# Layer 2's self attention in skewed steps with the norm by tile, and new arrangements of the mixtures' heads and of layer 1's weight rounding

## The chip, the cores and the metric

One core of a Trainium2 chip runs the whole program: four layers, each of a cross attention, a self attention and a feed-forward part, twelve stages in all. The metric is the device time of one execution in microseconds (us), lower is better; a time of the kernel is the median of several executions. The engines of the core run side by side and wait for each other by semaphores: PE (TensorE, matrix products and transposes; PEld is its weight load), DVE (VectorE), ACT (ScalarE), POOL (GpSimd) and SP (SyncE, which here only issues transfers). Each engine takes its instructions in order.

## What is computed

`x` has 16 x 64 tokens of 256 features, that is 1024 rows, and there is a context of 16 x 1601 rows. Every stage is `x = x + stage(layernorm(x), ...)`. The stages that the change touches are these:

```python
# layer 2, self attention (64 tokens of a batch see each other, causally)
q, k, v = x @ Wq, x @ Wk, x @ Wv
att = softmax(where(causal, q @ k.T / sqrt(256), -inf))
out = layer_norm(att @ v + v, gamma, beta)
return out @ Wfc + bfc
# layers 0 and 3: two of eight experts for each token; layer 2: one of eight
logits = x @ Wg.T            # layer 2: (x @ wg_red.T) @ unit(wg).T
gates, experts = top_k(softmax(logits))
out[token] += gate * expert(x[token])
# layer 1, feed-forward: weights and activations rounded
w1q, w2q = round(w1 / mean|w1|), round(w2 / mean|w2|)   # clipped to -1, 0, 1
y = bit_linear(silu(conv(bit_linear(x, w1q))), w2q)
```

## The kernel before

The 1024 rows lie as eight tiles of 128 rows (`NT = 8`), `self.x` and its normed copy `self.xn`. `run` (L2348) goes through the twelve stages; ahead of each it asks for the weights of this stage and of the next, afterwards it calls `normalise()`. The writer gives the instructions in program order, and a scheduler at build time sets the order on each engine. An instruction that goes through `pinned` (L193) while `self.fixed` is set stays behind everything written before it on its engine; others may move ahead. All PE work passes through `mm` (matrix product, L199) or `tr` (transpose, L203), so PE's rows carry one of these two lines.

**The norm.** When a stage has finished tile `t` of `x`, `ready(t)` (L299) takes mean and variance on DVE (`bn_stats`, `bn_aggr`), three small operations on POOL make the scale and the shift (L309 to L311, one of them a power), and `normalise` writes `xn` on ACT (L317), one tile later than it was measured. After the experts of a mixture all eight tiles come back from memory at once and `ready` runs for each in turn (L1591).

**Layer 2's self attention** (L1344) is written tile by tile without pins. All queries and keys are projected first; then for each tile: values, scores, maximum, exponential, transpose of the probabilities, product with the values. Then all eight outputs are normed (`layernorm`, L279), turned (`to_T`) and multiplied with `Wfc`.

**The head of a mixture.** `expert_rows` (L1593) stores `xn` in memory with one transfer and turns all of it; `gate_logits` (L1436) multiplies each tile with the gates; `top2`, `two_choices`, `places` and `slots` work out on DVE in which expert tile and row each token goes. `places` counts with a running sum of 16 additions (L1454), `slots` compares with a list of 128 row numbers 16 times (`R`, L1518) for 16 products on PE. `experts` (L1531) then has for each of 23 (layer 2: 15) expert tiles the weights `W` (three buffers, loaded by SP at an address read from `rows`), the tokens `xs` gathered by POOL from memory, two products, and a scattered addition to memory by POOL (L1578), one after the other. In this kernel the first three `W` are asked for as soon as `rows` is known.

**Layer 1's rounding.** `quant_weight` (L1766) rounds a weight matrix of 128 x 2048 numbers: a sum of absolute values on DVE (L1772), one small product, and three passes on ACT and DVE. For `w1` it is written as a whole at step 165 of layer 1's cross attention, which runs 227 steps of one key tile each; for `w2` in layer 1's self attention (L1336), into whose weight buffer `w2` is loaded at its start. The context tiles `ctxT` of the cross attentions go through two buffers of the pool `stream`.

## Time and profile before

| what | value |
|---|---|
| median of 3 runs | 3267.34 us (3263.81 to 3276.09) |
| the profiled execution | 3270.24 us, its span 3268.5 us |
| busy PE / ACT / DVE / POOL | 93% / 42% / 39% / 11% |
| granted PE clock, mean over the span | 0.952 |
| layer 1's cross attention, with its projections | 844 to 1699 us |
| layer 1's self attention, feed-forward | 1699 to 1773, 1773 to 1864 us |
| layer 2's cross attention, self attention | 1864 to 2366, 2366 to 2433.5 us |
| the head of layer 0's / 2's / 3's mixture | 602 to 652 / 2433.5 to 2469 / 3043.5 to 3082.3 us |
| the experts of layer 0 / 2 / 3 | 652 to 844 / 2469 to 2581 / 3082.3 to 3253 us |

The times of the stages are counted from the span's start, by where PE passes from one to the next. "Granted clock" is the share of its full rate at which PE was let run. In the profile's rows a name is `out<-in`, a row of the timeline is start, length, engine, line and operation, and the bracket at its end is the idle time of the engine before it and what ended it. A row of the stage table has the length, then for each engine its busy time and number of instructions, then the granted clock, the share of the DMA engines in use and GB/s. DMA is a transfer between memory and the chip.

### The profile page before, as it was taken

Reading aid. Unit: us, or ns where it says so; the run is one execution under the profiler, and the core shown is the slowest. Engines: PE = TensorE matmul, PEld = TensorE weight load, DVE = VectorE, ACT = ScalarE, POOL = GpSimd, SP = SyncE. Lnnn points to the kernel's source line nnn. Section 1 sums busy time; section 2 is a strip of 40 time slices with the busy share of each in tenths; the row PEclk is TensorE's granted clock in tenths of the full one; section 3 lists DMA queues with packets and bytes.
Section 4 is the critical chain, followed back from the end, with each engine's and each line's share of the span. In section 5 each row is a group of like instructions: output and inputs, shape, how many; then the busy total and the mean of one; then the engine's idle time right before and its main releaser. Section 6 shows DMA issues by size and latency. Waiting matters only on the chain. (4 is left out here: it accounts for less than half of the span.)

```text
span 3268.5 us, 67442 instructions
## 1 busy us (share of the span) xinstructions
PE 3028.5 (93%) x28567; PEld 2267.5 (69%) x28567; DVE 1261.3 (39%) x3415; ACT 1361.5 (42%) x2699; POOL 370.9 (11%) x538
## 2 busy tenths in 40 slices
PE   7999997699799999999998999999979798889798
PEld 5666664599566666666676777777748676778697
DVE  6888874422244444444446421121242100045200
ACT  5888884211233333333334522222222387753111
POOL 0000002223200000000010000000012311111132
PEclk9999998699899999999998999999988899999799
DMA  6334431389211121211257111111208555510497
GB/s 217 107 128 135 134 108 42 147 282 322 59 61 61 61 81 43 79 61 61 81 172 224 28 61 41 61 50 52 77 17 302 159 184 183 184 48 1 156 324 241
DMA packets 178362, 395.09 MB, mean 121 GB/s; under 512 B 11446, under 2 KB 142270, under 8 KB 165214
## 3 DMA queue, kind: packets, MB, share of 16 engines
q1 hardware_dynamic: 165070, 372.91, 33.1%
q0 software_dynamic: 11712, 16.00, 2.5%
q8 instruction: 225, 3.69, 0.5%
q10 hardware_dynamic: 1280, 1.88, 0.2%
q14 instruction: 75, 0.61, 0.1%
HBM read 375.02 MB, written 16.12 MB: 120 GB/s over the span
## 5 line engine op out<-in xcount | busy, mean ns | idle before, releaser
L199 PE MATMUL acc<-ctx,st 128*128 128x257 f32 (+1 forms) x1664 | 397.2, 383 | 0.0
L199 PE MATMUL pss<-qk,ctxT 128*128 128x512 f32 (+1 forms) x832 | 388.8, 592 | 0.6 <-DVE qk L634 0.6
L199 PEld LDWEIGHTS acc<-ctx,st 128*128 128x128 f32 (+1 forms) x1664 | 310.1, 190 | 94.6 <-issue 35.7
L459 DVE CUSTOM_DVE_ANT_0 Sx<-s,mneg 128x384 f32<-128x384 f32 (+1 forms) x512 | 264.2, 570 | 88.7 <-PE s L199 88.7
L650 DVE TENSOR_TENSOR top<-pss,top 128x512 f32<-128x512 f32 x192 | 132.7, 691 | 402.4 <-ACT st L645 402.3
L203 PE MATMUL pst<-cst,Sx 128*128 128x128 f32 (+1 forms) x1736 | 254.8, 286 | 26.1 <-ACT Sx L1381 10.2
L674 ACT ACTIVATE st<-st 128x512 f32<-128x512 f32 (+1 forms) x208 | 130.6, 629 | 292.4 <-DVE st L673 292.4
L935 ACT ACTIVATE Pr<-pss 128x512 f32<-128x512 f32 (+1 forms) x512 | 220.1, 523 | 60.2 <-PE pss L199 58.7
L503 ACT ACTIVATE PT<-pst 128x384 f32<-128x384 f32 x512 | 215.1, 489 | 63.6 <-PE pst L203 62.5
L203 PEld LDWEIGHTS pst<-cst,Sx 128*128 128x128 f32 (+1 forms) x1736 | 187.9, 142 | 73.6 <-ACT PT L503 27.8
L199 PEld LDWEIGHTS pss<-qk,ctxT 128*128 128x128 f32 (+1 forms) x832 | 154.1, 186 | 120.7 <-issue 102.7
L645 ACT COPY st<-pss 128x512 f32<-128x512 f32 (+1 forms) x208 | 121.6, 585 | 201.6 <-PE pss L199 201.6
L199 PE MATMUL pso<-W,hT 128*128 128x256 f32 x884 | 200.9, 379 | 0.0
L199 PE MATMUL pst<-wst,ctxT 128*128 128x256 f32 (+1 forms) x832 | 183.4, 380 | 0.0
L199 PE MATMUL psk<-ctxT,wst 128*128 128x512 f32 (+1 forms) x512 | 181.8, 513 | 0.8 <-ACT qT L797 0.8
L199 PEld LDWEIGHTS pso<-W,hT 128*128 128x128 f32 x884 | 163.2, 190 | 19.7
L199 PEld LDWEIGHTS pst<-wst,ctxT 128*128 128x128 f32 (+1 forms) x832 | 153.5, 186 | 25.9 <-issue 2.7
L199 PE MATMUL pss<-q,ctxT 32*128 32x128 f32 (+1 forms) x3328 | 152.2, 299 | 15.9 <-issue 13.1
L199 PEld LDWEIGHTS psk<-ctxT,wst 128*128 128x128 f32 x512 | 88.3, 190 | 93.7 <-issue 92.1
L199 PEld LDWEIGHTS pss<-q,ctxT 32*128 32x128 f32 (+1 forms) x3328 | 120.0, 193 | 47.8 <-issue 36.9
L356 POOL TENSOR_TENSOR x<-x,bvec 128x256 f32<-128x256 f32 x40 | 29.7, 744 | 1079.7 <-ACT xn L317 1079.7
L837 DVE TENSOR_TENSOR v<-pst,bvec 128x512 f32<-128x512 f32 (+1 forms) x112 | 73.1, 653 | 204.4 <-PE pst L199 204.4
(394 smaller groups left out, 4515.9 us busy)
## 6 DMA issues: line engine op xcount, KB each, us to landing
ctxT<-in_ctxT_dram SPq DMA_DIRECT2D x64, 1601.0 KB
W<-in_L_experts_dram SPq DMA_DIRECT2D x61, 1024.0 KB
ctx<-in_ctx_dram SPq DMA_DIRECT2D x32, 1536.0 KB
W<-in_L_experts_dram SPq DMA_DIRECT2D x23, 1536.0 KB
ctx<-in_ctx_ones_dram SPq DMA_DIRECT2D x16, 1632.0 KB
ctx<-in_ctx_one_dram SPq DMA_DIRECT2D x16, 1542.0 KB
W<-in_L_experts_dram SPq DMA_DIRECT2D x23, 768.0 KB
W<-in_L_experts_dram SPq DMA_DIRECT2D x15, 1028.0 KB
```

The source lines that it names most:

```text
L199: self.pinned(self.nc.tensor.matmul(out, lhsT, rhs, start=start, stop=stop))
L203: self.pinned(self.nc.tensor.transpose(out, in_, self.ident[:n, :n]))
L356: self.nc.gpsimd.tensor_tensor(self.x[:, t, :], self.x[:, t, :], self.bv(i), ALU.add)
L459: self.pinned(nc.vector.tensor_tensor_reduce(out=Sx[:, j, :n], in0=ps[j][:, :n], in1=st["mneg"][:, o : o + n], op0=ALU.add, op1=ALU.max, s ...
L503: self.pinned(nc.scalar.activation(PT, ps, AF.Exp))
L645: pin(nc.scalar.copy(st[:kn], ps[:kn]))
L650: pin(nc.vector.tensor_tensor(top[b][:kn], ps[:kn], top[b][:kn], ALU.max))
L674: pin(nc.scalar.activation(st, st, AF.Exp, scale=HD**-0.5))
L837: nc.vector.tensor_tensor(o, ps[:kn, :n, :], bv[:kn].to_broadcast([kn, n, D]), ALU.add)
L935: nc.scalar.activation(st["Pr"][:kn, g : g + n, j, :], ps[j][:kn, :n, :], AF.Silu)
```

## The change

1. `L2_attn` is written in 13 steps with lags and with its instructions pinned: in step `n` the scores of tile `n`, the last product of tile `n-5`, turning of `n-4`, norm of `n-3`, attention of `n-2`, transposing of `n-1`, values of tile `n`. The norm is by tile (POOL has three small operations for each). Transposes, projections and `add_bias` are pinned too.
2. `ready_all` norms the eight tiles after the experts of layers 0 and 2: two powers of four columns on POOL, and the writing of `xn` shared by ACT and DVE.
3. `gate_logits` goes tile by tile: store of the tile (eight transfers), turning, logits a step later. The last tile's `normalise` moves into it, at its fourth step; in front of layer 1's feed-forward it moves behind the first turning.
4. `top2` and `places` write in place (no copies), the running sum takes four doubling steps (three in layer 2), and `slots` makes `R` four at a time.
5. In `experts` only the first `W` is asked for at once; the row numbers of the others are read from `rest`, a copy made by POOL behind the first two gathers.
6. `quant_parts` spreads the five parts of a rounding over steps of layer 1's cross attention: `w1` from step 145, `w2` from step 203. `w2` is loaded there at step 196, into a `ctxT` buffer, which it keeps until layer 1's feed-forward is over. `add_bias(2)` moves to step 3.

```diff
+    def ready_all(self):
+        for h in range(2):
...
+            for i in range(4):
+                pin(nc.vector.bn_stats(st, self.x[:, 4 * h + i, :]))
+                pin(nc.vector.bn_aggr(mv[:, i, :], st))
+            pin(nc.vector.tensor_scalar(rs[:, 0], mv[:, :, 1], 1e-5, None, ALU.add))
+            nc.gpsimd.tensor_tensor(
+                rs[:, 0], rs[:, 0], self.c("pow")[:, 0:1].to_broadcast([P, 4]), ALU.pow)
+        for h, (mv, rs) in enumerate(parts):
+            pin(nc.vector.scalar_tensor_tensor(
+                rs[:, 1], mv[:, :, 0], -1.0, rs[:, 0], ALU.mult, ALU.mult))
+            for i in range(4):
+                if i % 2:
+                    pin(nc.vector.tensor_scalar(o, x, ...))
+                else:
+                    pin(nc.scalar.activation(o, x, AF.Identity, ...))
...
@@ L1_xattn
-                self.add_bias(2)
+                at(3, self.add_bias, 2)
-                    at(NKT * 12 + 9, self.quant_weight, pst, self.w1, "pst")
+                    for i, part in enumerate(self.quant_parts(pst, self.w1, "pst")):
+                        at(NKT * 11 + 2 + 2 * i, part)
+                    at(NKT * 15 + 1, self.load_w2)
+                    def ready_w2():
+                        for i, part in enumerate(self.quant_parts(pst, self.w2, "pst")):
+                            at(NKT * 15 + 8 + 2 * i, part)
+                    at(NKT * 15 + 7, ready_w2)
@@ L1_attn
-                        if n == 3:
-                            self.quant_weight(psa, self.held["L1_ffn"][1], "py")
@@ L2_attn
+            tc.tile_pool(name="l2a_t", bufs=4, space=PSUM) as pst,
+            tc.tile_pool(name="l2a_v", bufs=2, space=PSUM) as psv,
+            tc.tile_pool(name="l2a_o", bufs=1, space=PSUM) as pso,
+            self.fixed = True
...
+            for n in range(NT + 5):
+                for lag, fn in (
+                    (0, scores), (5, last), (4, back), (3, normal), (2, attend), (1, turn),
+                    (0, values),
+                ):
+                    if 0 <= n - lag < NT:
+                        fn(n - lag)
@@ places
-        for g in range(G):
-            nc.vector.tensor_tensor(cum[:, g + 1, :], cum[:, g, :], ps[:, g, :], ALU.add)
+        nc.vector.tensor_copy(cum[0][:, pad:, :], ps)
+        while step < G:
+            nc.vector.tensor_tensor(
+                cum[1][:, pad:, :], cum[0][:, pad:, :], cum[0][:, pad - step : pad - step + G, :],
+                ALU.add)
+            cum.reverse()
+            step *= 2
@@ slots
-        for g in range(G):
-            nc.vector.tensor_scalar(R, self.c("iota128"), lo[:, g : g + 1], None, ALU.is_equal)
-            self.mm(ps, R, V[:, :, g, :], g == 0, g == G - 1)
+        for g in range(0, G, 4):
+            nc.vector.tensor_tensor(R, ..., ALU.is_equal)      # 128 x 4 x 128
+            for i in range(4):
+                self.mm(ps, R[:, i, :], V[:, :, g + i, :], g + i == 0, g + i == G - 1)
@@ experts
-        got = [fetch(0), fetch(1)]
+        W, xs = {0: fetch(0, rows)}, [gather(0), gather(1)]
+        self.pinned(nc.gpsimd.tensor_copy(rest, rows))
+        W[1] = fetch(1, rest)
...
-            for t in range(NT):
-                self.ready(t)
+            self.ready_all()
@@ gate_logits
+        def turn(t):
+            nc.sync.dma_start(xin[t * P : (t + 1) * P, :], self.xn[:, t, :])
+            for kc in range(2):
+                self.tr(ps[:, kc, :], self.xn[:, t, kc * P : (kc + 1) * P])
+            pin(nc.scalar.copy(turned[t], ps))
...
+        for t in range(NT + 2):
+            if t < NT:
+                turn(t)
+            if 0 <= t - 1 < NT:
+                logits(t - 1)
+            if 0 <= t - 2 < NT:
+                reduced(t - 2)          # layer 2 alone: the second, small product
+            if t == 3:
+                self.normalise()
@@ L1_ffn
             turn_x(0)
+            self.normalise()
@@ run
-                self.normalise()
+                if after not in ("L0_ffn", "L1_ffn", "L2_ffn", "L3_ffn"):
+                    self.normalise()
```

## The prediction

> **What bounds the kernel now.** First the page: PE is busy for nearly all of the span, and the slices show where it isn't.
>
> ```profile
> PE 3028.5 (93%) x28567; PEld 2267.5 (69%) x28567; DVE 1261.3 (39%) x3415; ACT 1361.5 (42%) x2699; POOL 370.9 (11%) x538
> PE   7999997699799999999998999999979798889798
> PEclk9999998699899999999998999999988899999799
> ```
>
> 240 us of the span are without PE work, and the dips of both rows (slices of 82 us) lie at the mixtures' heads and in layer 2's self attention. So a saving counts where PE waits, and a change in layer 1's cross attention must only not disturb. Next, the stage table: length, then busy time of PE, weight load, DVE, ACT, POOL, then clock, DMA share, GB/s.
>
> ```profile
> 602.00:652.00 50.00, 25.75 (x179) 22.81 (x178) 24.52 (x95) 7.11 (x15) 8.81 (x18) 0.62 0.61 228
> 881.00:1699.00 818.00, 814.72 (x3554) 537.62 (x3552) 347.11 (x636) 299.90 (x522) 14.56 (x28) 1.00 0.21 69
> 2384.50:2433.50 49.00, 32.79 (x129) 25.57 (x128) 27.54 (x90) 8.44 (x28) 5.47 (x13) 0.79 0.00 0
> 2439.50:2444.00 4.50, 4.16 (x10) 1.36 (x11) 0.84 (x2) 0.94 (x2) 0.00 (x0) 0.50 0.80 262
> 2890.00:3043.50 153.50, 142.16 (x826) 121.09 (x817) 77.30 (x212) 59.89 (x127) 22.47 (x47) 0.97 0.00 1
> 3043.50:3082.30 38.80, 17.27 (x85) 16.04 (x85) 18.28 (x86) 3.26 (x5) 5.54 (x8) 0.56 0.60 226
> 3075.00:3082.00 7.00, 0.00 (x0) 0.00 (x0) 0.00 (x0) 0.00 (x0) 3.24 (x3) 0.50 1.01 416
> ```
>
> The heads of layers 0 and 3 keep PE half idle at a clock near 0.6; layer 2's tile loop waits for a third of 49 us at 0.79. Who it waits for, by the tile `Sx`:
>
> ```profile
>   DVE nm L1379: 24.0, 7
>   ACT Sx L1381: 22.1, 16
> ```
>
> Within a tile everything is a chain: scores, maximum, exponential, transpose, product. The period is 3.92 us, of which PE works 1.9.
>
> **Layer 2's self attention.** At full clock the trace has for a tile: values 0.87, scores 0.43, transpose 0.18, attention 0.43, two transposes 0.36, last product 0.87, in all 3.14 us (25.1 for eight tiles). ACT has 3.1 a step (exponential 0.58, norm 0.52, two turned copies 0.66, probabilities 0.27, values 0.37, waits between), DVE 2.85. Every product reads what an earlier step made, so a full step costs the larger plus little, 3.3. There are 13 steps: five of filling, whose chain scores, maximum, exponential takes 2.1 each (10.6), three full (9.9), five of emptying, in which the last tile goes through attention, statistics, POOL's 1.0, norm, turning and product (10): 30.5 us. I add 1.3 for a clock of 0.95 and 1.8 for 13 hand-overs of 0.14 (0.06 to 0.3 in the trace). Projections now end at 2383.04; pinned behind all transposes, whose last tile comes at 2369.8, they lose 1.0: 2384.05. PE so ends at 2417.6 instead of 2433.35: **15.7 us**. Of the new waits, `normal` on ACT waits for POOL, and behind it stand PT and the values' copy; POOL's three operations (1.01) follow a step earlier, with 1 us to spare. `add_bias` (8 x 0.72 on POOL) is done before step 5 needs `x`.
>
> A rule speaks against it. The row: the clock is 0.79 in the chained loop, 0.97 in layer 3's self attention, where PE is busy 142 of 153 us in skewed steps. The Trainium skill (TensorE: Matmul & The Clock Gate, "A second HAM failure mode: psum-queue depth-cycling") says that micro-idling between groups of products, with accumulators cycled in every iteration, is enough to make the clock oscillate. By the row the products cost 25.1 / 0.95 = 26.4 us, by the rule at 0.79 31.8, so 5.4 less gain: 10.3. At half clock throughout (50 us of products and 5 of waits) nothing is gained, the lower end; the upper, at full clock without hand-overs, is 18.8. I take the row: the new loop is of that form.
>
> **The heads of the mixtures.** Layer 3's, from the timeline (start, length), and its running sum:
>
> ```profile
> 3065.28 4.75 SPq L1545 DMA_DIRECT2D W<-in_L_experts_dram  x6
> 3067.05 7.09 PE L199 MATMUL pst<-V,R 128*128 128x69 f32 x32 [8.21 <-POOL V L1508]
> 3075.14 1.20 POOL L1547 DMA_INDIRECT xs<-l3i,token  x1 [8.15 <-DVE share L1528]
> 3082.28 0.66 PE L203 MATMUL pst<-cst,xs 128*128 128x128 f32 x2 [8.14 <-DMA xs<-l3i,token]
> ```
> ```profile
> L1454 DVE TENSOR_TENSOR cum<-cum,pst x16: 154/161/164, 3058.5 to 3061.5; 128x8 f32<-128x8 f32 x16
> ```
>
> The gather takes 7.1 us because three `W` of 2.1 MB fill the DMA engines (share 1.01 above). With one `W`, 5 us from about 3067, they are free when it starts; the next gather, at 3083.79, landed in 2.75, layer 2's third in 3.01. I take 3.4: **3.7**. Bounds: 0 if something else fills them, 4.4. Late next is then the transpose itself, as the first `W`, there at 3072, is ready before it. The second `W` waits for the copy `rest`, on POOL behind two gathers; then SP issues it 4.2 us after the first gather, it lands 9 to 10 after and is needed at 12.5. Behind it on SP only the other weights wait. Were this cover gone, each us late is an us lost.
> Sum: 16 additions are 3.16 us (3058.5 to 3061.66); a copy of 0.28 and four of some 0.32 (`place`, 128x128, takes 0.28) are 1.6, **1.6** gained. Copies left out, **0.2**. `R` four wide: the first takes 0.69 (a copy of 512 columns) instead of 0.28, **-0.3**; then PE bounds.
> Gates: PE's end 3043.4 to logits 3054.4 is 11.1 us, transposes 3.5, then products 6.6, at half clock. By tile PE has 2.4 + 6.6, and 1.1 at the ends: 10.1, **1.0** gained (bounds -0.4 and 2.6). `normalise` at the fourth step, some 4 us in, finds its scale ready at 3046.0.
> Layer 3: 1.0 + 0.2 + 1.6 + 3.7 - 0.3 = **6.2**. Layer 0 has the same with a gather of 6.7 (3.4 gained) and 1.5 more, as the rounding's sum goes from between its `R`:
>
> ```profile
> 636.38 2.28 DVE L1772 TENSOR_REDUCE wa<-wst 128x1 f32<-128x2048 f32 x1
> 638.91 5.39 PE L199 MATMUL pst<-V,R 128*128 128x69 f32 x24 [1.49 <-DVE R L1518]
> ```
>
> 1.0 + 0.2 + 1.6 + 3.4 - 0.3 + 1.5 = **7.4**. In layer 2, PE's end to logits is 15.1; eight tiles of 1.35 and 1.5 at the end are 12.3, and 0.2 from the sum: **3.0**. Its gather is covered by PE's products until 2469.
>
> The store: the row above at 2439.5 is layer 2's, 1 MB at 262 GB/s. The skill (DMA: Bandwidth & Descriptors, "Measured (HBM→SBUF, 128 partitions, SWDGE, issued from GpSimd)") wants a MiB or more in a transfer for 75% of the peak; here it becomes eight of 128 KB. At a quarter of the row's rate that is 16 us, spread over the gates; from the last one's issue to the gather lie some 20 us of DVE work. So 0 by both; without that cover up to 12.
>
> **The norm after the experts.** Layer 0's, by the tile `rs`:
>
> ```profile
> L310 POOL TENSOR_TENSOR rs<-rs,cst x8: 540/548/572, 852.1 to 862.8; 128x1 f32<-128x1 f32 x8
>   ACT xn L317: 19.2, 8
> ```
>
> Eight rounds of three POOL operations (1.0) and DVE's two take 13.4 us from `x` at 850.9 to the last `xn` at 864.4. New: eight statistics of 0.6 (4.9), a power of four columns (no row; between 0.55 and 4 x 0.55, taken as 0.8), shift, then four `xn` on each of two engines (ACT 0.6): 9.3. Transposes follow: 4.1 earlier, less 0.4 for the end: **3.7** (2 to 5). `add_bias` stood between on POOL and now comes at step 3. Layer 2 takes 10.3 and gains **1.3**.
>
> **The rounding.** In layer 1's cross attention (PE 814.7 of 818 us) a step is 3.44 us. The parts were 2.28 (sum), 0.32, 2.10 (ACT), 1.23 and 1.29 us; DVE's share of the stage is 42%, ACT's 37%, so each fits into the 2 us left in a step, with two steps for each part: 0. If all were exposed, 2 x 6.9 = 13.8 lost. Layer 1's self attention gains its own 0.6 of stall, and its feed-forward **1.4**, as the copy of `xT` (1776.34) no longer stands behind the last `xn` (1775.83). The load of `w2` holds a `ctxT` buffer until about 1860, so layer 2's second `ctxT` comes then instead of 1660; needed at 1898, it has 38 us for 5. In between stand, behind that wait on SP, `ctx` loads that nothing reads. If what frees the buffer came 38 us later, PE would wait for it, us for us.
>
> **Sum**: 7.4 + 3.7 + 0.6 + 1.4 + 15.7 + 3.0 + 1.3 + 6.2 = 39.3. Profiled execution 3270.2 - 39.3 = 3230.9; it lies 2.9 above the median, which gives **3228**.
>
> **Rivals.** (a) The clock: as above 5.4 lost in layer 2's attention, or, in lockstep of ACT and DVE, up to 11, and gates at half clock by tile 2 worse each: 3245 (17%). (b) `W` held back comes late: no gain at the gathers (7.1) and 3 us of stall at three heads: 3267.3 - 39.3 + 16 = 3244 (10%). (a) with (b): 3261 (5%). (c) Slower: the scattered additions become the bound of the experts.
>
> ```profile
> L1578 POOL DMA_INDIRECT l3o<-y,token x22: 1549/1584/1634, 3094.4 to 3249.8; - x22
>   DMA l3o<-y,token: 79.3, 18
> ```
>
> Each waits for the one before to land; their interval is 7.27 us beside PE's 7.24. If the shifted loads of `W` lengthen landing (6.4 median, 9.7 at most) by 0.93 for 58 intervals, 54 are lost: 3282. It decides from 39.3 / 58 = 0.68 on. Against it: in steady state a load starts when a buffer comes free, as now (8%). (d) Better: gates at full clock, attention near its upper end: 3215 (10%). The forecast keeps 50%.
>
> A change under 0.5% (16.3 us) can't be told from none. Faster holds the forecast, (a), (b), (d), less what of (a) and (b) goes beyond 3251: 82%; same 10%, slower 8%. The range reaches from (d) to the worse half of (a) with (b): 3211 to 3258; the forecast's own is 3219 to 3237.
>
> **What the profile after would show.** PE's end of layer 2's attention about 34 us after its projections, clock over 0.9; first gathers landing in 3 to 4 us at a DMA share below 1; running sum under 2 us; no rounding sum among layer 0's `R`; two powers of POOL ahead of layer 1 and the last `xn` some 9 us after `x`; PE's pace in layer 1's cross attention unchanged. It is wrong if ACT paces the 13 steps, if `W` is late at the second tile, or if the experts' interval grows.

## The result, and the profile after

The changed kernel takes 3238.79 us (median of 4 executions, 3233.65 to 3246.37) beside 3271.72 us of the kernel before (4 executions in the same series): ratio 0.9908, interval 0.9885 to 0.9932. A second series gave 3233.92 beside 3266.12, ratio 0.9893 (0.9860 to 0.9927). So the change is worth 1%, 33 us, against 39.3 forecast; both medians lie in the range of 3211 to 3258, 6 and 11 us above the 3228 of the forecast.

The profiled execution has a span of 3233.9 us, 34.6 less than before. First its page:

```profile
span 3233.9 us, 67553 instructions
PE 3017.9 (93%) x28591; PEld 2264.5 (70%) x28591; DVE 1255.3 (39%) x3369; ACT 1371.5 (42%) x2741; POOL 363.9 (11%) x517
PE   7999998699899999999998999999989798889798
PEclk9999998699999999999998999999978899999799
```

The dips of both rows are fewer but lie where they did: at the mixtures' heads and behind layer 2's self attention. The stage table shows why; columns as before (length, busy time of PE, weight load, DVE, ACT and POOL, granted clock, DMA share, GB/s):

```profile
608.00:645.00 37.00, 19.88 (x92) 17.79 (x93) 15.02 (x61) 4.98 (x14) 7.18 (x12) 0.56 0.51 171
865.50:1686.30 820.80, 815.64 (x3557) 538.10 (x3556) 353.74 (x642) 301.76 (x523) 9.23 (x21) 1.00 0.21 68
2368.20:2399.00 30.80, 27.14 (x137) 21.25 (x135) 20.28 (x69) 22.97 (x65) 14.95 (x45) 0.92 0.08 26
2399.00:2437.10 38.10, 30.70 (x110) 18.93 (x110) 16.08 (x65) 5.64 (x13) 5.23 (x8) 0.50 0.29 100
2399.00:2416.50 17.50, 16.95 (x65) 9.68 (x65) 4.46 (x19) 3.53 (x10) 1.00 (x3) 0.50 0.05 16
3015.00:3050.00 35.00, 18.02 (x87) 16.39 (x86) 15.09 (x65) 4.87 (x11) 5.09 (x8) 0.55 0.30 103
3045.50:3049.60 4.10, 0.05 (x1) 0.00 (x0) 0.69 (x4) 0.00 (x0) 2.56 (x4) 0.50 0.12 32
```

Layer 2's tile loop (third row) went from 49.4 to 31.0 us, PE busy 27 of 31. But layer 2's head (fourth row) takes 38.1 us instead of 35.6, at a clock of 0.50 from end to end, although PE is busy 30.7 us of it. The row below that is its first part, the gates. The same head before, at 0.65:

```profile
2433.50:2469.00 35.50, 24.02 (x86) 13.73 (x86) 16.50 (x66) 6.22 (x11) 8.31 (x19) 0.65 0.38 138
```

Stage by stage, by the ends of PE's work in the two profiled executions (a gain is positive):

| stage | before | after | gain | forecast |
|---|---|---|---|---|
| start to layer 0's last attention product | 611.1 | 609.2 | 1.9 | 0 |
| head of layer 0 | 40.9 | 34.2 | 6.7 | 7.4 |
| experts' end to layer 1's first `qT` product | 37.0 | 30.5 | 6.5 | 3.7 |
| rest of layer 1's cross attention | 818.5 | 820.8 | -2.3 | 0 |
| layer 1's self attention | 73.8 | 70.8 | 3.0 | 0.6 |
| layer 1's feed-forward | 85.8 | 82.6 | 3.2 | 1.4 |
| layer 2's cross attention | 507.0 | 507.0 | 0 | 0 |
| layer 2's self attention, to its first scores | 18.1 | 21.3 | -3.2 | -1.0 |
| the same, its tile loop | 49.4 | 31.0 | 18.4 | 16.7 |
| head of layer 2 | 35.6 | 38.1 | -2.5 | 3.0 |
| experts' end to layer 3's first scores | 20.8 | 20.5 | 0.3 | 1.3 |
| layer 3's self attention | 150.4 | 155.6 | -5.2 | 0 |
| head of layer 3 | 38.9 | 34.6 | 4.3 | 6.2 |
| the experts of three layers, layer 3's cross attention, the last stores | | | 3.5 | 0 |

What the prediction said the profile would show is mostly there. The first gather of layer 3, from its issue (second row) to the transposes (third row):

```profile
3038.49 7.07 PE L199 MATMUL pst<-V,R 128*128 128x69 f32 x32 [7.26 <-DVE V L1609]
3046.55 1.20 POOL L1652 DMA_INDIRECT xs<-l3i,token  x1 [8.42 <-DVE share L1630]
3049.63 0.66 PE L203 MATMUL pst<-cst,xs 128*128 128x128 f32 x2 [4.08 <-DMA xs<-l3i,token]
```

3.1 us instead of 7.1, at a DMA share of 0.12 (last row of the stage table). PE's products with `R` still take 7.1 us, at half clock. The running sum, the power for four tiles, and the scattered additions, each from the view of its tile:

```profile
L1549 DVE TENSOR_TENSOR cum<-cum x4: 291/292/293, 3031.2 to 3032.1; 128x128 f32<-128x128 f32 x4
```
```profile
L330 POOL TENSOR_TENSOR rs<-rs,cst x2: 1051/1116/1182, 844.9 to 847.3; 128x4 f32<-128x4 f32 x2
```
```profile
L1687 POOL DMA_INDIRECT l3o<-y,token x23: 1549/1584/1634, 3061.7 to 3220.9; - x23
```

The four additions take 0.29 each; the power of four columns takes 1.1 us (0.8 was assumed); the scattered additions come every (3220.9 - 3061.7) / 22 = 7.24 us, which is PE's pace of before: the experts did not slow down (layer 3's take 170.5 us in both).

Two more views tell of waits that the prediction did not have. At the start of layer 3's self attention, the last tile's norm on POOL; the first row is the same wait of PE in the kernel before:

```profile
2896.59 0.55 PE L203 MATMUL ps<-cst,xn 128*128 128x128 f32 x3 [1.35 <-ACT xn L317]
```
```profile
2859.92 1.64 PE L203 MATMUL ps<-cst,xn 128*128 128x128 f32 x13 [0.52 <-DVE x L401]
2860.03 3.46 POOL L392 TENSOR_TENSOR x<-x,bvec 128x256 f32<-128x256 f32 x5
2863.44 0.19 POOL L311 TENSOR_TENSOR rs<-mv,cst 128x1 f32<-128x1 f32 x1
2866.47 0.48 PE L203 MATMUL ps<-cst,xn 128*128 128x128 f32 x1 [4.92 <-ACT xn L353]
```

Five pinned bias additions, 3.46 us, stand on POOL ahead of the norm's three small operations (two more come between them), and PE waits 4.92 us for `xn` (1.35 before). And in layer 1's cross attention the first part of the rounding stands ahead of what reads a batch's accumulators:

```profile
1404.79 2.27 DVE L1924 TENSOR_REDUCE wa<-wst 128x1 f32<-128x2048 f32 x1
1407.58 0.23 DVE L727 RECIPROCAL rec<-acc 128x1 f32<-128x1 f32 x2
1408.74 0.44 PE L203 MATMUL pst<-cst,Z 128*128 128x128 f32 x2 [1.82 <-ACT Z L732]
```

### The profile page after: what moved, and what is told of

Read it like the earlier page. It is cut to its first block, busy times and chain, and to the rows that moved or that the text cites. A ratio compares the mean times of both kernels' runs of the same rounds, so it can differ in the third digit from the quotient of the medians.

```text
span 3233.9 us, 67553 instructions
## 1 busy us (share of the span) xinstructions
PE 3017.9 (93%) x28591; PEld 2264.5 (70%) x28591; DVE 1255.3 (39%) x3369; ACT 1371.5 (42%) x2741; POOL 363.9 (11%) x517
## 5 line engine op out<-in xcount | busy, mean ns | idle before, releaser
L311 POOL TENSOR_TENSOR rs<-mv,cst 128x1 f32<-128x1 f32 x80 | 17.3, 217 | 1494.5 <-DVE mv L307 1414.2
L199 PE MATMUL pss<-q,ctxT 32*128 32x128 f32 (+1 forms) x3328 | 148.1, 295 | 16.9 <-issue 13.5
L199 PEld LDWEIGHTS pss<-q,ctxT 32*128 32x128 f32 (+1 forms) x3328 | 117.3, 189 | 47.9 <-issue 37.0
```

What stands on the lines that cost most here:

```text
L199: self.pinned(self.nc.tensor.matmul(out, lhsT, rhs, start=start, stop=stop))
L311: nc.gpsimd.tensor_tensor(rs[:, 0:1], mv[:, 1:2], self.c("eps"), ALU.add)
```

## The experiments

**Does the attention carry its gain alone?**

```diff
 (the kernel before)
-    def L2_attn: tile by tile, no pins, norm behind all tiles
+    def L2_attn: as in the changed kernel; everything else as before
```

> The kernel before with the first part of the change alone (layer 2's self attention in 13 skewed, pinned steps; add_bias as before). My theory: this part carries the gain of its stage by itself. From the last product of layer 2's cross attention to the last product of its self attention 67.5 us become 52 to 53 (projections end 21 us after the start, then 31 us of steps at a clock over 0.9), all other stages keep their lengths, and the time falls by 15 us, ratio 0.9955. Rival A (the slow clock at the attention's end is handed on): the head of layer 2, in its arrangement of before, runs at a clock of 0.5 throughout and takes 40 us instead of 35.5, so that 10 us are left. Rival B (the gain needs the other parts): the stage stays above 58 us.

3255.54 us beside 3268.19, ratio 0.9959 (0.9945 to 0.9972; 10 executions): 13 us. The loop and the head behind it:

```profile
2387.90:2417.30 29.40, 25.33 (x139) 20.57 (x138) 20.31 (x69) 22.38 (x64) 14.83 (x45) 1.00 0.00 1
2417.30:2448.60 31.30, 20.85 (x87) 12.83 (x85) 16.46 (x64) 4.49 (x7) 5.25 (x9) 0.71 0.43 156
```

The stage takes 47.7 us (18.3 to the first scores, 29.4 for the loop), better than the 52 to 53 expected: here the loop runs at a clock of 1.00. So the part carries its stage alone, and rival B falls. Rival A was not put to the test: the clock was up at the end of the attention, so there was no slow clock to hand on, and the head came down to 31.2. (In the profile of the changed kernel above the clock was down there, and the head took 38.1 at 0.50.) Stage and head together gain 24 us in this profile, the whole only 15. Against the gain stand two stages whose instructions are those of the kernel before: layer 3's self attention took 157.0 us instead of 150.4, and layer 1's 82.5 instead of 73.8. The latter, before and in this run:

```profile
1699.20:1773.00 73.80, 64.25 (x645) 48.38 (x645) 49.14 (x112) 22.18 (x38) 12.26 (x27) 0.79 1.06 325
```
```profile
1693.40:1776.00 82.60, 74.43 (x645) 56.90 (x645) 50.52 (x114) 22.95 (x39) 12.97 (x28) 0.66 0.93 289
```

The same 645 instructions of PE, 8.7 us apart, and PE busy 10.2 us longer at the lower clock. What follows therefore compares stages, and reads the clock beside each.

**The gates in the order of before.**

```diff
 (the changed kernel, gate_logits)
+        if name in ("l0", "l2", "l3"):
+            self.normalise()
+            nc.sync.dma_start(xin[:NTOK, :]..., self.xn)      # one store
+            self.to_T(pst, "pst", self.xn, xnT)
+            ...                                               # then all products, one copy
-        for t in range(NT + 2): turn(t); logits(t - 1); reduced(t - 2)
```

> The changed kernel with one part undone: in the three heads the rows go to memory in one transfer, all tiles are turned and then multiplied with the gates, as before. My theory: the new order by tile costs layer 2 and layer 3 time, since its small products at half clock stand between the transposes. PE's end of the attention to the first logits copied whole goes back from 17.5 to 15 us in layer 2, from 12.0 to 11.1 in layer 3, and from 11.7 to 12.0 in layer 0; the head of layer 2 (to the first transposed expert rows) from 38.1 to 35.6; 3 us less in all. Rival (the slow clock comes from the end of the self attention and not from the order of the gates): layer 2's head stays at a clock of 0.5 and at 38 us or more with the old order too.

One execution, 3226.89 us. From PE's last attention product to the last product of the logits: layer 0 11.8 us (changed kernel 11.5), layer 3 9.2 (11.8), layer 2 10.2 (17.5), and layer 2's head 30.6:

```profile
2398.00:2428.60 30.60, 21.34 (x85) 13.02 (x85) 15.28 (x54) 4.48 (x7) 5.40 (x9) 0.72 0.43 151
```

Less than the 35.6 expected, since the head began at full clock. The run alone can't tell the order from the clock; the following ones can: with the new order and the clock up, layer 2's gates take 11.6 us, so that at equal clock the order costs layer 2 some 1.3, and the clock the other 6. In layers 0 and 3 the clock falls during the gates, and how early it falls moves them too. Where it falls equally late, the new order gains 0.3 in layer 0 (11.5 us beside 11.8, fall after 3.2 and 3.3) and loses some 0.5 in layer 3 (11.3 and 11.4 beside 10.8 to 11.0, fall after 4.6 to 4.8).

The rival is not settled by this. In layer 2's gates the order of before has eight instructions of PE with 512 columns where the new order has 32 with 128. In each of the three executions with the old order in which the clock was down there (the kernel before and the two runs with four edits, below), it was back 2.5 to 3.2 us after the first with 512; with the new order and no filler it came back in one of four. So part of those 6 us may come from the order after all, by way of the clock; no run here takes the two apart.

**Weights asked for at once.**

```diff
-        W, xs = {0: fetch(0, rows)}, [gather(0), gather(1)]
-        rest = sp.tile(...); self.pinned(nc.gpsimd.tensor_copy(rest, rows))
-        W[1] = fetch(1, rest)
+        W, xs, rest = {}, [], rows
+        for i in range(2):
+            W[i] = fetch(i, rest); xs.append(gather(i))
```

> The changed kernel with one part undone: the first three W of each mixture are asked for as soon as the row numbers are known. My theory: the first gather then shares the transfer engines with three W again; from its issue to the transposes on PE it takes 6.7 us in layer 0 (3.2 with the change) and 8 in layer 3 (4.1 with it), the heads grow from 34.2 to 37.6 and from 34.6 to 38.6 us, layer 2's is unchanged, and the time rises by 7.5 us. Rival (what shortened the gather is the store in eight transfers or the earlier end of the first W): the gathers stay under 5 us.

3242.75 us (one execution). Layer 3's first gather again, issue and end:

```profile
3048.36 1.20 POOL L1652 DMA_INDIRECT xs<-l3i,token  x1 [8.42 <-DMA W<-in_L_experts_dram]
3055.58 0.66 PE L203 MATMUL pst<-cst,xs 128*128 128x128 f32 x2 [8.22 <-DMA xs<-l3i,token]
```

7.2 us, and the heads are 38.1 (layer 0) and 38.6 us (layer 3), 3.9 and 4.1 more than with the change. At the gathers the theory holds with its numbers, and the rival falls. The total, forecast to rise by 7.5, is 4 to 9 us above the medians of the changed kernel, within what its executions spread. Layer 2's head, where the weights don't matter, came out at 32.1 instead of 38.1:

```profile
2400.30:2432.40 32.10, 24.40 (x110) 15.56 (x109) 16.07 (x65) 6.07 (x13) 5.18 (x8) 0.71 0.32 119
```

The same 110 instructions of PE as in the changed kernel, busy 24.4 us instead of 30.7, at a clock of 0.71 instead of 0.50.

**Dense work in layer 2's head.** It adds products that nobody reads.

```diff
             if t < NT: turn(t)
+            if t < NT and name == "l2":
+                for k in range(2):
+                    self.mm(junk, self.xn[:, t, k * P : (k + 1) * P], self.xn[:, t, :])
             if 0 <= t - 1 < NT: logits(t - 1)
```

> The changed kernel with work added whose result nobody reads: in layer 2's head two products of 128 x 128 by 128 x 256 for each of the eight tiles (0.43 us each at full clock, 0.86 at half). The question is why PE's clock stays at 0.5 in that head for 47.8 us though PE is busy 17.0 of 17.5 us there. Theory 1: transposes and narrow products don't count as work for the clock. Then the filler brings the clock to 1.0 some 7 us into the head; gates take 20 us instead of 17.5, what follows 15 instead of 20.6, and the head about 35 instead of 38.1. Theory 2: the clock is down for a time of its own after the gaps at the end of the self attention, whatever PE does. Then the clock stays at 0.5 and the head takes 13.8 us more, 52.

3235.5 us (one execution). The head takes 38.9 us, close to the 38.1 of the changed kernel:

```profile
2400.30:2439.20 38.90, 31.41 (x142) 21.17 (x141) 16.08 (x65) 5.70 (x13) 5.24 (x8) 0.76 0.27 98
```

It has 32 instructions more and needs 0.8 us more, not 13.8, at a clock of 0.76 instead of 0.50. In the record of the clock it fell to 0.5 at 2395.5, before the head, as in the changed kernel (2394.2), and was back at 1.0 at 2402.4, not at 2442.0; in the idle time ahead of `R` it fell again, at 2422.8. So theory 2 in its form (0.5 throughout, 52 us) did not come true. But theory 1 is not shown either: in the next run the clock came back at 2402.0 without any filler, and stayed up through the gates as well. What this run does show is that nothing is gained where PE itself is the bound and has to do the filler too.

**The same kernel once more.**

> The changed kernel once more, unaltered. Three traces with the same instructions around layer 2's self attention differ: its first scores come 18.4 or 21.3 us after the cross attention, the head after it takes 32.1 or 38.1 us. My theory: the clock is decided in windows whose position against the program is chance, so an execution falls on one side or the other. This execution then has one of these two pairs again or a mixture, each with a clock that goes with it (1.0 up to the middle of the head, or a drop inside the gap of 2.7 us before the last transposes and from the attention's last step on), and executions spread over 10 us. Rival (the neighbouring edits decide, not chance): 21.3 and 38.1 within 0.3 us again. Ratio to the kernel before: 0.9905.

3233.92 us (3226.16 to 3239.26), ratio 0.9893. First scores after 19.8 us, head 33.4:

```profile
2397.50:2430.90 33.40, 25.85 (x110) 15.99 (x110) 16.10 (x65) 5.59 (x12) 5.23 (x8) 0.65 0.32 114
```

A third pair for the same instructions, between the two others and with a clock between them: one program gives different pairs in different executions, and the rival (the neighbouring edits decide) falls. All profiled executions that have both stages unaltered, with the clock of the head:

| execution | to the first scores, us | head, us | its clock |
|---|---|---|---|
| changed kernel | 21.3 | 38.1 | 0.50 |
| the same again | 19.8 | 33.4 | 0.65 |
| weights at once | 18.4 | 32.1 | 0.71 |
| norm as before | 18.4 | 32.1 | 0.71 |
| rounding as before | 21.3 | 38.1 | 0.50 |

**The norm after the experts, as before.**

```diff
         if name != "l3":
-            self.ready_all()
+            for t in range(NT):
+                self.ready(t)
```

> The changed kernel with one part undone: after the experts of layers 0 and 2 each tile is measured and normed in turn, with three operations on POOL for each. My theory: the norm for all tiles at once is what brings layer 1's first products with qT from 37.0 us after the experts' end to 30.5; undone, they go back to 36 to 37, and layer 3's first scores from about 18.5 (17.4 and 20.5 seen) to 19 to 21; the time rises by 6 to 8 us. Rival (the gain comes from the bias additions, which no longer share POOL with the norms, since they are now at step 3): undone, layer 1's start stays near 31 us.

3236.73 us (one execution). My theory fell: from the experts' end to layer 1's first `qT` product it takes 31.9 us, not 37. That stretch in this kernel and in the changed one:

```profile
835.60:867.50 31.90, 20.02 (x50) 9.07 (x50) 8.56 (x23) 7.61 (x13) 14.67 (x33) 0.73 0.15 37
```
```profile
835.00:865.50 30.50, 17.52 (x51) 8.74 (x50) 11.91 (x31) 4.99 (x9) 9.35 (x11) 0.78 0.15 39
```

The ten executions with `ready_all` take 30.1 to 32.0 us there, so 31.9 without it lies among them: what it is worth can't be seen. The rival came true. In this stretch the run differs from the kernel before only in the bias additions, which now stand at step 3, so they account for 4 to 5 of the 6.5 us (36.3 and 37.0 us in two executions of the old order): before, one of 0.72 us stood on POOL between the norms of two tiles, and where it did `xn` came every 1.7 to 1.8 us; here one comes every 0.9 to 1.2. Layer 3's first scores come 18.9 us after the experts, within the 17.6 to 20.5 of the changed kernel: there it is worth nothing that can be seen.

**Four edits to the changed kernel.**

```diff
 # 1 L2_attn: each half of the tiles turned, then projected
+            for h in range(2):
+                (turn tiles 4h to 4h+3); (project them)
 # 2 L1_xattn
-                        at(NKT * 11 + 2 + 2 * i, part)
+                        at(NKT * 11 + 5 + 2 * i, part)
 # 3 add_bias
-            self.pinned(self.nc.gpsimd.tensor_tensor(...))
+            self.nc.gpsimd.tensor_tensor(...)
 # 4 gate_logits of layers 2 and 3 in the order of before
```

> The changed kernel with four edits, each read in its own stage. (1) Layer 2's projections of the first four tiles stand before the transposes of the last four: PE's gap of 2.7 us goes, first scores come 16.5 to 17.5 us after the cross attention whatever the clock's windows, instead of 18.4 or 21.3. (2) Layer 1's first rounding sum comes three steps later, off the step in which the accumulators of a batch are read: the cross attention takes 818.5 us instead of 820.8. (3) add_bias without pins: before layer 3's self attention the last tile's norm no longer waits behind bias additions on POOL, PE's gap there goes from 4.9 to 1.5 us. (4) Gates of layers 2 and 3 in the order of before: 10.3 us instead of 11.6 (17.5 at half clock) in layer 2, 9.2 to 10.8 instead of 11.8 in layer 3. By my theory 1.5 to 4 + 2 + 3 + 2 = 8.5 to 11 us less than the changed kernel, some 3229. Rival: each only moves a wait and the sum is within 3 us of the changed kernel.

3221.89 us (3210.69 to 3224.64), ratio 0.9846 (0.9812 to 0.9880), 12 less than the changed kernel in the same series (8.5 to 11 were expected). (1) First scores after 16.9 us, as expected. (2) 822.3 us for the cross attention, not 818.5; aligned product by product with the kernel before, the loss of 2.0 us at 1408.7 is gone and one of 0.8 has come at 1429.9, while some 3 went in its first six microseconds, to a clock still at 0.5. Half right. (3) POOL and PE at the start of layer 3's self attention:

```profile
2853.20 0.33 POOL L311 TENSOR_TENSOR rs<-mv,cst 128x1 f32<-128x1 f32 x1 [0.79 <-DVE mv L307]
2855.36 0.55 PE L203 MATMUL ps<-cst,xn 128*128 128x128 f32 x3 [1.35 <-ACT xn L353]
```

PE's wait is back at 1.35 us. From the last transpose of the stage before to the last of these it takes 4.1 us as in the kernel before, and 8.0 in each of nine executions with pinned bias additions: 3.9 us, the same each time. (4) Gates 11.8 us in layer 2 and 11.0 in layer 3; in layer 2 the clock had dropped, so it says little.

**Filler in the idle time of the heads.**

```diff
+    def fill(self, n):          # products that nobody reads
+        for k in range(n):
+            self.mm(junk, self.xn[:, k % NT, :P], self.xn[:, k % NT, :])
 # after the logits (layers 0, 3): fill(3); after the running sum's products: fill(8)
 # after the products with R (layers 0, 3): fill(6)
```

> The changed kernel with products added that nobody reads (128 x 128 by 128 x 256), where PE waits for DVE in the mixtures' heads: three after the logits of layers 0 and 3, eight after the two products of the running sum, six after the products with R of layers 0 and 3. My theory (the clock counts wide products, not narrow ones, and PE's idle time in the heads costs nothing else): the clock is at 1.0 when the products with R begin, they take 3.6 us instead of 7.1, layer 2's products with the bias 3.6 instead of 7.3, and the first expert tile runs at full clock (3 us less): 6 us less for each head, 15 to 18 in all, about 3222. Rival (the filler delays what stands behind it on PE by as much as the clock gives, or the clock stays down): within 4 us of the changed kernel, or up to 10 slower.

3216.66 us (3214.91 to 3218.59), ratio 0.9843 (0.9814 to 0.9871): 17 less than the changed kernel in the same series. The heads of layers 0, 2 and 3:

```profile
608.80:641.20 32.40, 25.58 (x120) 21.80 (x118) 14.92 (x60) 4.07 (x11) 5.04 (x9) 0.74 0.53 182
2386.90:2415.60 28.70, 24.91 (x126) 16.23 (x125) 15.94 (x65) 6.07 (x13) 5.39 (x9) 0.91 0.30 100
2997.10:3031.70 34.60, 28.66 (x119) 24.64 (x119) 15.10 (x65) 4.87 (x11) 5.40 (x8) 0.65 0.30 107
```

The size of the whole was right, its place only in part. In the heads of layers 0 and 3 the clock was back at full rate 2.9 us (layer 0, 621.7) and 5.7 us (layer 3, 3014.5) after the filler began. Layer 0's head by stretches of the clock, and the one stretch at half clock that the changed kernel has in its place (its head ends at 643.4):

```profile
614.90:621.70 6.80, 6.19 (x22) 4.95 (x21) 2.75 (x15) 0.95 (x3) 0.00 (x0) 0.50 0.95 315
621.70:628.60 6.90, 4.17 (x20) 3.40 (x20) 6.05 (x28) 0.00 (x0) 0.09 (x1) 0.99 0.00 1
628.60:638.80 10.20, 8.84 (x37) 8.51 (x38) 4.15 (x10) 0.00 (x0) 1.76 (x2) 0.50 0.62 231
```
```profile
612.40:649.90 37.50, 21.21 (x95) 19.87 (x95) 13.43 (x53) 4.64 (x10) 5.68 (x6) 0.50 0.56 198
```

In none of eleven executions without filler did the clock come back there: once down in layer 0's head it stayed at 0.5 for 34 to 44 us, until 4 to 7 us of the experts were done. So that the filler brings it back in these heads is shown. That it does so by its width, as theory 1 has it, is argued: the products with `R`, 69 columns wide, keep PE busy for 7 us on end in the changed kernel and did not bring it back, but narrow filler in the same idle time was not tried. In layer 0 `R` still took 7.07 us: the eight products were through too early, and the clock fell again in what was left.

Where is the gain? Beside the executions without filler, gathers as in the change, layer 0's head is 1.7 to 2.2 us shorter, layer 3's not at all. The experts, whose first tile now runs at full clock, take 188.8 us in layer 0 (190.2 to 191.6) and 167.5 in layer 3 (169.2 to 170.5). Layer 2's head takes 28.7, but its filler stands behind the gates, which ran at full clock already: beside the 32.1 of executions with the same luck it is 3.4. That makes 8 to 11 us; the other 6 to 9 between the medians (four executions each) lie in stages without filler, and what brought them is not shown.

**The rounding as before** (its passes stay pinned, unlike those of the kernel before).

```diff
-                    (the five parts of w1 from step 145; load of w2 at step 196, its parts from 203)
+                    at(NKT * 12 + 9, self.quant_weight, pst, self.w1, "pst")
 # L1_attn
+                        if n == 3:
+                            self.quant_weight(psa, self.w2, "py")     # w2 is loaded at the start of L1_attn
```

> The changed kernel with one part undone: w1 is rounded as a whole at step 165 of layer 1's cross attention, w2 is loaded at the start of its self attention and rounded there. My theory, from the stages: the cross attention loses 2.05 us to the first sum in the changed kernel, the self attention gains 2.7 us at its rounding and more where the clock then stays up (68.0 to 72.6 us in six executions of the changed kernel and its relatives, 73.8 and 82.5 in two with the old rounding). Undone: the cross attention's loss at the first sum is gone, the self attention takes 73 to 83 us, the total rises by 1 to 8 us. Rival (the part only moves the same work, and the clock's chance made the difference): self attention within 68 to 72.6 us, the total the same or lower by 2.

3243.7 us (3235.07 to 3247.59), ratio 0.9916 (0.9891 to 0.9942). Self attention 75.3 us, within the theory's span and outside the rival's. The cross attention did not get shorter but longer, 827.2 us: pinned in one piece the rounding lost 3.9 us at its sum (1491.6) and 1.8 more, as the clock fell there; some 3 went at its start, to a clock still at 0.5. By the ratios to the kernel before it is 3 to 8 us worse than the changed kernel, but the intervals overlap, so the total doesn't tell; only the stalls at the two roundings can be put down to the part.

**The attention without pins.**

```diff
             V, Sx, tot, out, rs, oT = {}, {}, {}, {}, {}, {}
+            self.fixed = False
```

> The changed kernel with one part undone: layer 2's self attention is written in the same 13 skewed steps, but without pins after the projections, so that the scheduler may order it. Changed kernel: 29.4 to 31.0 us from the first scores to the last product. My theory: it is the written order with its lags that breaks the chain of a tile, and what the pins add is small: 29 to 34 us. Rival (the scheduler pulls the steps of a tile together again, as it did before): 42 us or more, against 49.4 of the kernel before.

3235.39 us (one execution):

```profile
2361.00:2396.50 35.50, 27.36 (x138) 20.45 (x136) 18.88 (x69) 23.00 (x65) 14.83 (x45) 0.99 0.07 23
```

The loop takes 35.5 us, 1.5 above the theory's span and far from the rival's 42. First scores come after 16.3 us instead of 18.4 to 21.3, as the scheduler puts the first projections ahead of the last transposes. Together they take 51.8 us, the changed kernel's instructions 47.9 to 52.8. So the written order with its lags breaks the chain (35.5 us instead of 49.4); the pins give 4 to 6 us in the loop and lose 2 to 5 ahead of it, and whether they gain anything in all stays open.

**Mends and more filler together.**

```diff
 # the four edits, and:
+ fill(4) after the logits, fill(14) (layer 2: 12) after the running sum's products, fill(6) after R
```

> The changed kernel with the four edits of the earlier run and more filler in the heads: four products after the logits of layers 0 and 3, fourteen (layer 2: twelve) after those of the running sum, so that PE is busy until the products with R begin, and six after these. In the run with eight the clock fell to 0.5 again in the idle time left before R (628.6 in layer 0, 3021.3 in layer 3), and R took 7.1 us. My theory: now R runs at full clock, 3.6 us, without a later start, and the two sets of edits add up: the heads of layers 0 and 3 at 29 to 31 us, of layer 2 at 28; about 3203 us, ratio 0.981. Rival 1: the filler holds up R by what the clock gives, heads no shorter than with eight (32.3, 28.7, 34.6), about 3209. Rival 2: products with R are too narrow to keep the clock, R at 7 us all the same, about 3208.

3210.46 us (3204.96 to 3211.67), ratio to the kernel before 0.9818 (0.9799 to 0.9836). This beats both kernels, 58 us under the one and some 25 under the other, though not by the 3203 expected. Layer 0's products with `R`, its first gather and its end, and the three heads:

```profile
631.64 3.87 PE L199 MATMUL pst<-V,R 128*128 128x69 f32 x32 [0.75 <-DVE V L1617]
636.52 1.31 POOL L1662 DMA_INDIRECT xs<-l0i,token  x1 [5.24 <-DVE share L1640]
639.60 0.44 PE L203 MATMUL pst<-cst,xs 128*128 128x128 f32 x2 [1.45 <-DMA xs<-l0i,token]
```
```profile
608.40:639.60 31.20, 26.85 (x134) 23.19 (x132) 14.92 (x60) 4.07 (x11) 4.96 (x9) 0.78 0.56 190
2388.50:2419.60 31.10, 26.85 (x109) 16.77 (x109) 15.20 (x54) 4.49 (x7) 5.40 (x9) 0.79 0.40 140
2990.70:3019.40 28.70, 24.30 (x133) 21.02 (x133) 15.38 (x60) 3.26 (x5) 4.61 (x8) 0.88 0.43 151
```

`R` takes 3.87 us instead of 7.07, so rival 2 falls. Layers 0 and 3 are at 31.2 and 28.7, where the theory wanted 29 to 31; layer 2 is at 31.1, not 28: the clock fell at 2413.5 and was down under the last products of the head. The two sets of edits add up to some 25 us of the 29 that they gave singly; beside the four edits alone the heads and experts are 12 us shorter in the profiles.

## Why the prediction was right, and where it was not

**What it had right.** The order of sizes, and the three largest steps by their own working. The tile loop: 30.5 us at full clock were worked out; 29.4 to 29.5 were measured in seven executions at full clock, 30.4 to 31.5 in four where it fell before the end. The 1.8 for hand-overs was not needed. The projections' loss of 1.0 was 0.3 at full clock and 3.2 in the profiled execution. The gathers: 3.4 and 3.7 forecast, 3.4 (16.6 to 11.3 us from the start of `R` to the transposes, less 1.8 for `R`) and 4.1 measured, and undone by one edit. The running sum: 1.6 forecast; in layer 3 from its first operation to `place` 3.1 us before, 1.7 after. The layer 0 rounding sum between the `R`: 1.5 forecast, 1.8 measured. The store in eight parts was covered, as forecast: in layer 3 the last part was issued at 3019.7, 27 us ahead of the gather. Rivals (b) and (c) did not occur: no tile waited for `W` at the second place, and the additions to memory kept PE's pace. Of rival (a) the half on the attention did not come; the half on gates by tile at half clock, 2 worse each, did in layer 2 (2.6) and in part in layer 3 (1.0).

**Weighing row against rule** went the row's way for the loop itself: 0.92 to 1.00 there, not 0.79, so 15 to 20 us were gained and not 10.3. The loss came elsewhere. The Trainium skill's warning of a clock that oscillates with micro-idling (TensorE: Matmul & The Clock Gate, "A second HAM failure mode: psum-queue depth-cycling") was weighed for the loop alone. In four of the eleven executions the clock did fall in the loop's last steps, where PE waits between the groups of a tile; whether by that rule is not shown. The loop lost 1 to 2 us by it, but the head behind it up to 6: there transposes and narrow products keep PE busy 97% of the gates' time (16.95 of 17.50 us, fifth row of the stage table) and the clock still stayed at 0.5.

**The step that failed: "eight tiles of 1.35 and 1.5 at the end are 12.3"**, set against the 15.1 of before, and with it the 1.0 for the gates of layers 0 and 3. The 12.3 was not the fault: at full clock the new order takes 11.6 us in layer 2. But at full clock the old one takes 10.2 to 10.5; the 15.1 held some 4.5 us of slow clock, which the prediction took for a cost of the order. At half clock the new order takes 17.5, 2.1 for each tile, as each tile's transposes, product, copy and second product follow each other. In layers 0 and 3 it takes 11.3 to 12.3 (10.1 once), the old order 9.2 to 11.8. So gates by tile gain 0.3 in layer 0 at best and lose in the two others. For the three heads 4.8 were forecast (1.0, 1.0 and 2.8); the profiled execution lost 3.3 (+0.3, -1.0, -2.6). Where the clock held, layer 2's gates still took 1.3 more than the old order at that clock.

**Missed: a pin on the bias additions.** The prediction named POOL behind the last norm and asked only who waits for the additions, not what they pass. They passed the last tile's norm ahead of layer 3's self attention: 3.9 us. The other 1.3 lost in that stage lie within what the clock moves there (150.4 us in one execution of the old code, 157.0 in another). That the pin is the cause is shown by taking it off (third of the four edits): the wait went back to 1.35.

**Mis-sized: the norm after the experts.** 3.7 forecast, 5.7 to 6.5 found, and for another reason than the one put first: the bias additions that left POOL, not the batched norm. Its power takes 1.1 us and not 0.8, it lets the first transposes start 3 us later (13.0 us after the experts instead of 10.0), and with it undone nothing was lost. **The rounding**, put at 0 with up to 13.8 lost, cost 2.0 at one place: two steps for each part were room enough on average, but the first part fell on the very step in which a batch's accumulators are read. Against it, layer 1's self attention and feed-forward gained 6.2 where 2.0 were forecast. Aligned product by product, 2.7 of it come at the place where `w2` was rounded (1747 to 1758 before) and 1.5 at the first `xT`; the remainder goes with the clock (0.83 instead of 0.79 in the self attention). In the feed-forward it is steady: 82.5 to 82.8 us in all eleven executions with the change, 85.8 and 86.6 in two without it. In the self attention how much of it is chance stays open: 68.2 us in the second execution of the changed kernel, 82.5 in one of the old code.

**Luck.** Added up for the profiled execution: the three heads, by their gates, -8.1 against the forecast, layer 3's self attention -5.2, the first rounding sum -2.3, the two norms +1.8, layer 1's self attention and feed-forward +4.2, layer 2's self attention -0.5, and +5.4 from stages put at 0: 39.3 becomes 34.6. That the total came so near is in part luck: 16.1 us of losses met 11.4 of gains that were not forecast or not in this size, and nothing in the working ties the one to the other.

## What to carry to other kernels

A granted clock in one profile can be a property of that execution and not of the code (0.50, 0.65 and 0.71 in layer 2's head, same instructions): before a stage is costed by it, work out the old and the new order at the same clock, once at full and once at half. Pinning an instruction that nobody waits for can still cost, when it passes one that somebody does; read the engine's order at the seams between stages. Where PE idles for another engine anyway, wide products that nobody reads were worth some 10 us here by the stages that they bear on, about a third of what the whole change gave.

## What the runs showed of the hardware

In the heads of layers 0 and 3 the products with 8 columns, the transposes and `R` with 69 columns never brought the clock back (11 executions). Three to five products of 256 columns, put where PE idled, did each time, 2.9 to 5.7 us after the first of them (two kernels, both heads); in two of the four cases they ran on in the next batch of filler, with the products of the running sum between. In layer 2's head, with the gates by tile, it came back by itself in one execution and stayed down for 44.4 to 47.8 us in three others, with PE as busy: why, stays open. Stretches of half clock last multiples of 3.41 us (6.83, 10.24, 23.89, 47.79), at a position against the program that differs between executions of one kernel. Single stages with the same instructions differed by 6 to 10 us (layer 3's cross attention took 285.9 to 296.2 us in the profiled executions), and four executions of one kernel by 12 to 18. Of the ten executions with the attention alone the slowest (3266.1 us) had a mean clock of 0.950, the fastest (3242.6) one of 0.954. In the two kernels with filler the executions lay closer, 3.7 and 6.7 us apart.
